# Turning attention probabilities through DRAM instead of on the matrix engine

## The chip, the cores and the metric

One core of a Trainium2 chip runs the kernel. It has a matrix engine (PE, TensorE; its weight loads are listed as PEld), VectorE (DVE), ScalarE (ACT), GpSimd (POOL) and SyncE (SP), each with its own instruction stream, which it works through in order, and 16 DMA engines. The metric is the time of one execution on the device in microseconds (us), the median of several runs.

## The reference

A gated cross-attention followed by a gated mixture of experts, all in float32. x is 8 batches of 256 tokens of width 256, the context 8 batches of 120 rows.

```python
x = x + tanh(g_xattn[0]) * xattn(layernorm(x), ctx_1024, w_q, w_kv, w_out, b_out)
x = x + tanh(g_ffn[0]) * ffn(layernorm(x), W1, W2, Wr)

# xattn: 16 heads of 64
attn = einsum('bnhd,bmhd->bhnm', q, k) * 64 ** -0.5
attn = softmax(attn, axis=-1)
out = einsum('bhnm,bmhd->bnhd', attn, v).reshape(b, n, INNER) @ w_out + b_out

# ffn: 8 experts of width 1024, the 2 best of each token, weighted
h = silu(einsum('btd,efd->btef', x, W1)); y = einsum('btef,edf->bted', h, W2)
out = einsum('bte,bted->btd', gate, y)
```

## The kernel before

There are two phases. **Attention** (up to about 272 us of the span) runs a loop of 32 units, line 1101. Unit s is a batch b (8 of them), a half o of the heads (8 heads) and a half nb of the batch's tokens (128), and k = 2 o + nb is its place in the batch. **Experts** (the rest) first takes one tile of 128 tokens for each expert (the "first" tiles), then full tiles and quarters; the order is the list at line 1061.

A unit's attention goes through these steps. `scores` (line 549) multiplies queries and keys into a PSUM tile psc of two banks, takes the maximum of each of 8 heads on VectorE (line 563), scales it by the negated score factor (line 569), and lets ScalarE write the exponentials into pr, with their sums in sm (line 575). `divide` (line 582) takes the reciprocal of the sums and multiplies pr by it, both on VectorE. `turn_pr` (line 588) turns pr, whose partitions are tokens, into pT, whose partitions are context rows: 8 transposes on PE against an identity matrix into two PSUM tiles tr (line 594), and two copies by ScalarE (line 595). `weigh(b, o)` (line 597) multiplies values by pT for both token halves (tile po), and `wide_out` (line 615) multiplies its result by the output weights (tile pw) for half of the tokens.

The order of the work on PE, VectorE, ScalarE and SP is the order in which the program writes it down (`manual_schedule`, line 417); GpSimd's is not written by hand. In iteration s of the loop, PE gets: the scores of unit s+1; at k=0 `weigh(b-1, 1)`, at k=2 `weigh(b, 0)` and half of the wide_out of the batch before; a part of the projections of queries, keys and values for the next batch (`project_q`, tile pq; `project_k` and `project_kk`, tile pk, copied to kT by VectorE; `project_v`, tile pv); at k=1 the other half of the wide_out and, in every second batch from 3 on, the router's logits (tile plT); at the end the 8 transposes of unit s itself. So the turning of a unit stands right ahead of the scores and the weighing of the next iteration. At k=0 `turn_y` and at k=3 `turn_x` turn normalized rows on PE (tiles lnT), and VectorE copies them; that copy is the last thing VectorE does in iteration k=0, and adding wide_out's result to x (line 626) the last at k=2.

The router's lists lie in DRAM (`routed`, 8 lists of 2048 rows of 265 numbers, one list for an expert). At the start SP fills each of them with empty rows, one transfer for a list of 2.1 MB (line 438). `places` (line 302) computes the rows of tokens and sends them there by indirect DMAs from GpSimd (line 366), two for each step of a generator, from iteration 14 on. Experts' weights are loaded into a buffer w_sb of 8 slabs, one for an expert, each loaded by `load_expert` (line 407) as two DMAs of 1 MB; before they come, the slabs hold attention's weights and intermediate tiles (lines 99 to 105). Expert 0 is loaded at the end of batch 2, 1 of batch 3, 2 of batch 4, and 6, 5, 4, 3 and 7 at the end of attention and in the first iterations of the expert loop. `load` (line 810) brings a first tile by nine DMAs on SP (lines 845 and 852), and the four iterations of the last batch load four of them.

PSUM has 8 banks: two for tr, two for psc (one buffer), four for the projections.

Of the kernel before, what the change touches and what calls it, by code (L numbers as in the profile page):

```python
# [9 lines left out]
F32 = mybir.dt.float32  # L10
I32 = mybir.dt.int32
AF = mybir.ActivationFunctionType
# [37 lines left out]
def tile_gated_xattn_moe(  # L50
# [22 lines left out]
    fp = ctx.enter_context(tc.tile_pool(name="ffn", bufs=2))  # L73
    ps_tr = ctx.enter_context(
        tc.tile_pool(name="ps_tr", bufs=2, space=bass.MemoryType.PSUM)
    )

    attention = ExitStack()
    ap = attention.enter_context(tc.tile_pool(name="attn", bufs=2))
    ps_big = attention.enter_context(  # L80
        tc.tile_pool(name="ps_big", bufs=1, space=bass.MemoryType.PSUM)
    )
# [5 lines left out]

    routed = tc.dram_tile([E * T + P, XW], F32, name="routed")


# [8 lines left out]
    v_sb = [w_sb[:M, 4, ts(i, INNER)] for i in range(2)]  # L100
    pT_sb = part(4, 2 * INNER, 8, N)[:M]
    qT_sb = [part(5, i * IC * N, IC, N) for i in range(2)]
# [39 lines left out]
    for e in range(E):  # L142
        nc.vector.memset(octal[:, e : e + 1], float(E**e))
    empty = w_sb[:, 2, :XW]
    nc.vector.memset(empty, 0.0)
# [156 lines left out]
    def places(g, rows, picked, bank):  # L302
# [56 lines left out]
        for h in range(2):  # L359
            for slot, oh in zip(slots, (oh1, oh2)):  # L360
# [4 lines left out]
                for i in range(2 * h, 2 * h + 2):  # L365
                    send = nc.gpsimd.indirect_dma_start(  # L366
                        out=routed[:, :],
                        out_offset=bass.IndirectOffsetOnAxis(
                            ap=slot[:, i : i + 1], axis=0
                        ),  # L370
                        in_=rows[h][:, i % 2, :],
                        in_offset=None,
                    )


                    for other in sends:
                        tc.declare_no_dep(
                            send.ins, other.ins, reason="each row of a list is sent once"
                        )

                    for first in firsts if g >= EARLY else []:
                        tc.declare_no_dep(
                            send.ins, first.ins, reason="rows behind those of the first tiles"
                        )
                    sends.append(send)
                    if g >= EARLY:
                        behind.append(send)
                yield


    ctxT_sb = ap.tile([P, DC, B * M], F32, name="ctxT_sb", bufs=1)

    x_v = x.rearrange("(n p) d -> p n d", p=P)
# [42 lines left out]
    nc.sync.dma_start(wr_sb[:, :, :E], wrT.rearrange("(c p) e -> p c e", p=P))  # L436
    for e in range(E):
        nc.sync.dma_start(
            routed[ts(e, T), :].rearrange("(n p) w -> p n w", p=P),
            empty.unsqueeze(1).to_broadcast([P, NBLK, XW]),  # L440
        )
    nc.sync.dma_start(routed[ds(NOWHERE, P), :], empty)

# [77 lines left out]
    def project_q(b, xnT, h):  # L521
        pq = ps_mm.tile([P, 2, N], F32, tag="mm", name=f"pq_{b}_{h}")
        for i in range(2):
            for c in range(DC):
# [6 lines left out]
                )  # L531
        nc.scalar.copy(qT_sb[b % 2][:, ts(h, 2), :], pq)

# [15 lines left out]
    def scores(u):  # L549
# [3 lines left out]
        for i in range(4):  # L553
            for j in range(2):
# [6 lines left out]
                )  # L561
        mx = small.tile([P, 8], F32, tag="mx", name=f"mx_{b}_{o}_{nb}")
        nc.vector.tensor_reduce(  # L563
            mx.rearrange("p (j i) -> p j i", i=4),
            psc[:, :, : 4 * M].rearrange("p j (i m) -> p j i m", m=M),
            AX.X,
            ALU.max,
        )
        nc.vector.tensor_scalar(mx, mx, -QK_SCALE, None, ALU.mult)  # L569
        pr = ap.tile([P, 8, M], F32, tag="pr", name=f"pr_{b}_{o}_{nb}", bufs=3)  # L570
        sm = small.tile([P, 8], F32, tag="sm", name=f"sm_{b}_{o}_{nb}")
        for j in range(2):
            for i in range(4):
                h = 4 * j + i
                nc.scalar.activation(  # L575
                    pr[:, h, :], psc[:, j, ts(i, M)], AF.Exp,
                    bias=mx[:, h : h + 1], scale=QK_SCALE,
                    accum_out=sm[:, h : h + 1],
                )
        return pr, sm  # L580

    def divide(pr, sm):
        nc.vector.reciprocal(sm, sm)
        nc.vector.tensor_tensor(  # L584
            pr, pr, sm.unsqueeze(2).to_broadcast([P, 8, M]), ALU.mult
        )

    def turn_pr(u, pr, sm):

        b, o, nb = u  # L590
        for j in range(2):
            tr = ps_tr.tile([P, 4, P], F32, tag="tr", name=f"tr_{b}_{o}_{nb}_{j}")
            for i in range(4):
                nc.tensor.transpose(tr[:M, i, :], pr[:, 4 * j + i, :], ident)  # L594
            nc.scalar.copy(pT_sb[:, ts(j, 4), ts(nb, P)], tr[:M, :, :])  # L595

    def weigh(b, o, ps_mm):

        for h in range(2):
            po = ps_mm.tile([P, 2, N], F32, tag="mm", name=f"po_{b}_{o}_{h}")  # L600
            for k in range(2):
                i = 2 * h + k
                for j in range(2):
                    nc.tensor.matmul(
                        po[ts(j, DH), k, :],
                        lhsT=v_sb[b % 2][:, ts(2 * (4 * o + i) + j, DH)],
                        rhs=pT_sb[:, 4 * j + i, :],
                        start=True,
# [472 lines left out]

    idle = ps_tr.tile([P, 4, P], F32, tag="tr", name="idle")
    for _ in range(10):
# [7 lines left out]
    for h in range(2):  # L1091
        project_q(0, xnTs[0], h)
    prs = {0: scores(units[0])}
    project_k(0, 1)()
    norm_x(1)
    project_q(0, xnTs[0], 2)
    project_v(0, 0)
    divide(*prs[0])
    nc.scalar.activation(tg, tg, AF.Tanh)

    for s, (b, o, nb) in enumerate(units):
        k = 2 * o + nb
        n = b + 1
        g = b // 2 - 1
        routing = b > 1 and b % 2 == 1
        if s + 1 < len(units):
            prs[s + 1] = scores(units[s + 1])

        if s == 0 or k == 2 and b + 2 < B:
            norms_x.finish()  # L1110
        if k == 0 and b > 1:
            norms_y.finish()
        if k == 1 and b + 2 < B:
            if b > 1:
                xs[b + 2] = load_x(b + 2)
            norm_x(b + 2)
        if k > 1 and b > 0:
            norm_y(b - 1, k - 2)


        copies, sums = [], []
        if k == 0 and b > 0:
# [4 lines left out]
        if k == 2:  # L1127
            weigh(b, 0, ps_mm)
            if b > 0:
                sums.append(wide_out(b - 1, 1, ps_mm))  # L1130
        if k == 0:
            project_q(b, xnTs[b], 3)
            if n < B:
                project_v(b, int(b == 0))
        elif n < B:
            project_q(n, xnTs[n], k - 1)
        if k == 1:
            copies += next_k(b, 0)
            if routing and n < B:
# [3 lines left out]
            if routing and n == B:  # L1143
                lg = next(lg)
        if k == 3:
            copies += next_k(b, 1)
            if b > 0:
                project_v(b, 1)
            if n == B - 1:
                project_v(n, 0)  # L1150
        if b == 1 and k % 2 == 0:
            copies.append(project_kk(2, k))
        for copy in copies:
            copy()
        if s + 1 < len(units):
            divide(*prs[s + 1])
        if k == 0 and b > 1:
# [25 lines left out]
        if n == B and k == 3:  # L1183
            open_tile(order[0], xts[0])
            picked[g] = router(g, lg)
        turn_pr((b, o, nb), *prs.pop(s))
        if k == 3 and b + 2 < B:
            turn_x(b + 2)
        if s == 0:
            turn_x(1)  # L1190
        if k == 3 and b in (2, 3, 4):
            load_expert(b - 2)
        if k == 3 and n == B:
            load_expert(6)
# [4 lines left out]


    for name, kw in (
        ("fw", {}),
# [146 lines left out]
```

## Time and profile before

| What | us |
|---|---|
| median of 3 runs (535.99 to 539.37) | 538.03 |
| profiled execution | 538.17 |
| its span | 536.5 |

| Engine | in the attention phase, 150 to 180 us | whole span |
|---|---|---|
| PE | 30.00 of 30 | 520.5 (97%) |
| VectorE | 18.03 | 285.0 (53%) |
| ScalarE | 16.57 | 219.4 (41%) |
| GpSimd | 7.93 | 127.4 (24%) |

The span is the time from the first to the last instruction of the profiled execution. Busy times are sums of an engine's instructions. PE's instructions overlap one another, so that the time that a group of matmuls takes from the rest is better read from the distance between the starts of groups than from their durations. In an answer on the order of time each line has start, duration, engine, line of the program, operation, output and input tiles and count, and in brackets how long the engine had been idle before it and what ended that. In groups by line the numbers behind the count are busy time, mean ns of one, and idle time before them with what ended it.

### The profile page before, as it was taken

The page shows a single profiled execution, that of the slowest core. Times are in us where ns is not written, and L with a number is a line of the kernel's source. Part 1 is how long each engine was busy: PE and PEld are TensorE (multiplying, and loading weights), DVE is VectorE, ACT ScalarE, POOL GpSimd, SP SyncE. Part 2 cuts the span into 40 slices and gives each one's busy share as a digit, 9 for nine tenths or more (in the row PEclk, how much of TensorE's full clock was granted, in tenths as well). Part 3 has the DMA queues.
Part 4 walks back from the last instruction along what each step waited for, and adds up shares of the span by engine and source line. Part 5 has one row for each costly group of instructions (what it writes and reads, how often), then busy time and mean ns, then how long its engine had stood idle before and what let it go on. Part 6 is the DMA issues. An engine that isn't in the chain of part 4 may idle for free. (4 is left out here: it accounts for less than half of the span.)

```text
span 536.5 us, 10501 instructions
## 1 busy us (share of the span) xinstructions
PE 520.5 (97%) x3636; PEld 439.3 (82%) x3636; DVE 285.0 (53%) x683; ACT 219.4 (41%) x700; POOL 127.4 (24%) x135
## 2 busy tenths in 40 slices
PE   8999999999999999999999999899999999999992
PEld 7788887878878788787889998799997787889991
DVE  3675656567765577644673446344544454443530
ACT  1666546464654655557530302011144555601110
POOL 2011100000332003310013446122331224333332
PEclk9999999999999999999999999899999999999998
DMA  8999990140521501012059784333332221332321
GB/s 295 336 305 306 309 254 21 49 148 2 169 88 35 184 1 40 32 47 35 2 179 375 224 244 74 42 42 44 48 44 32 31 33 16 49 36 26 43 28 20
DMA packets 82157, 57.58 MB, mean 107 GB/s; under 512 B 42864, under 2 KB 77168, under 8 KB 82096
## 3 DMA queue, kind: packets, MB, share of 16 engines
q1 hardware_dynamic: 75200, 47.36, 32.0%
q0 software_dynamic: 6480, 8.81, 9.1%
q10 hardware_dynamic: 416, 0.66, 0.4%
q8 instruction: 30, 0.49, 0.4%
q14 instruction: 31, 0.25, 0.2%
HBM read 28.67 MB, written 28.27 MB: 106 GB/s over the span
## 5 line engine op out<-in xcount | busy, mean ns | idle before, releaser
L575 ACT ACTIVATE pr<-psc,mx 128x120 f32<-128x120 f32 x256 | 88.2, 370 | 65.4 <-DVE mx L569 63.3
L897 PEld LDWEIGHTS ph_full<-xT_full,w 128*128 128x128 f32 x736 | 86.6, 195 | 8.7 <-issue 7.4
L897 PE MATMUL ph_full<-xT_full,w 128*128 128x128 f32 x736 | 88.5, 279 | 2.3 <-DVE xT_full L884 2.0
L913 PE MATMUL py_full<-w,hT_full 128*128 128x256 f32 x368 | 83.1, 379 | 0.0
L913 PEld LDWEIGHTS py_full<-w,hT_full 128*128 128x128 f32 x368 | 68.2, 190 | 8.4
L905 ACT ACTIVATE hT_full<-ph_full 128x1024 f32<-128x1024 f32 x23 | 23.5, 1022 | 98.0 <-PE ph_full L897 92.0
L525 PE MATMUL pq<-xnT,w_sb 128*128 128x256 f32 x256 | 62.7, 388 | 0.4 <-DVE xnT L208 0.4
L938 POOL DMA_INDIRECT out_dram<-y_full,xt_full x23 | 39.2, 1705 | 100.1 <-DVE y_full L921 69.9
L619 PE MATMUL pw<-w_sb 128*128 128x256 f32 x256 | 58.5, 382 | 0.0
L575 ACT ACTIVATION_READ_ACCUMULATOR pr<-psc,mx 128x1 f32 x256 | 55.5, 217 | 0.0
L525 PEld LDWEIGHTS pq<-xnT,w_sb 128*128 128x128 f32 x256 | 46.6, 190 | 10.8 <-issue 3.1
L619 PEld LDWEIGHTS pw<-w_sb 128*128 128x128 f32 x256 | 47.7, 190 | 9.0 <-issue 2.5
L563 DVE TENSOR_REDUCE mx<-psc 128x8 f32<-128x960 f32 x32 | 37.0, 1156 | 31.4 <-PE psc L555 31.4
L366 POOL DMA_INDIRECT routed<-rows,slot x32 | 31.9, 995 | 55.6 <-DVE slot L362 48.9
L921 DVE TENSOR_SCALAR y_full<-py_full,gate 128x256 f32<-128x256 f32 x23 | 11.1, 484 | 60.3 <-PE py_full L913 54.9
L595 ACT COPY w_sb<-tr 120x512 f32<-120x512 f32 x64 | 34.6, 596 | 20.0 <-PE tr L594 20.0
L584 DVE TENSOR_TENSOR pr<-pr,sm 128x960 f32<-128x960 f32 x32 | 37.1, 1158 | 1.1
L555 PE MATMUL psc<-kT,w_sb 64*128 64x120 f32 x512 | 37.2, 284 | 0.0
L985 ACT COPY part<-w_sb 128x1024 f32 x32 | 31.0, 1043 | 13.5 <-PE py_q L1024 13.0
L555 PEld LDWEIGHTS psc<-kT,w_sb 64*128 64x128 f32 x512 | 31.1, 187 | 6.4 <-issue 3.6
L864 DVE COPY w<-w_sb 128x2048 f32 x23 | 29.0, 1259 | 12.0 <-issue 4.9
L594 PEld LDWEIGHTS tr<-ident,pr 128*120 128x120 f32 x256 | 29.5, 138 | 5.7 <-issue 3.1
(173 smaller groups left out, 648.8 us busy)
## 6 DMA issues: line engine op xcount, KB each, us to landing
routed<-w_sb SPq DMA_DIRECT2D x8, 2120.0 KB
w_sb<-in_w1T_dram SPq DMA_DIRECT2D x8, 1024.0 KB
w_sb<-in_w2T_dram SPq DMA_DIRECT2D x8, 1024.0 KB
xt_full<-routed SPq DMA_DIRECT2D x184, 16.0 KB
out_dram<-x SPq DMA_DIRECT2D x8, 256.0 KB
x<-in_x_dram SPq DMA_DIRECT2D x7, 256.0 KB
w_sb<-in_w_kv_dram SPq DMA_DIRECT2D x3, 512.0 KB
w_sb<-in_w_q_dram SPq DMA_DIRECT2D x2, 512.0 KB
```

Of the source, the lines that this page charges most:

```text
L366: send = nc.gpsimd.indirect_dma_start(out=routed[:, :], out_offset=bass.IndirectOffsetOnAxis(ap=slot[:, i : i + 1], axis=0), in_=rows[h][: ...
L525: nc.tensor.matmul(pq[:, i, :], lhsT=wq_sb[:, c, ts(2 * h + i, P)], rhs=xnT[:, c, :], start=(c == 0), stop=(c == DC - 1),)
L555: nc.tensor.matmul(psc[:, j, ts(i, M)], lhsT=qT[ts(j, DH), 4 * o + i, ts(nb, P)], rhs=kT[ts(j, DH), 4 * o + i, :], start=True, stop=True,)
L563: nc.vector.tensor_reduce(mx.rearrange("p (j i) -> p j i", i=4), psc[:, :, : 4 * M].rearrange("p j (i m) -> p j i m", m=M), AX.X, ALU.max,)
L575: nc.scalar.activation(pr[:, h, :], psc[:, j, ts(i, M)], AF.Exp, bias=mx[:, h : h + 1], scale=QK_SCALE, accum_out=sm[:, h : h + 1],)
L584: nc.vector.tensor_tensor(pr, pr, sm.unsqueeze(2).to_broadcast([P, 8, M]), ALU.mult)
L595: nc.scalar.copy(pT_sb[:, ts(j, 4), ts(nb, P)], tr[:M, :, :])
L619: nc.tensor.matmul(pw[:, :D], lhsT=oT_sb[b % 2][:, ci, ts(k, P)], rhs=wo_sb[:, ci, :], start=(ci == 0), stop=(ci == IC - 1),)
L897: nc.tensor.matmul(ph[:, f, :], lhsT=w1[:, c, ts(f, P)], rhs=xT[:, c, :], start=(c == 0), stop=(c == DC - 1),)
L913: nc.tensor.matmul(py[:, :D], lhsT=hT[:, f, :], rhs=w2[:, f, :], start=(f == 0), stop=(f == FC - 1),)
L938: add = nc.gpsimd.indirect_dma_start(out=out[:, :], out_offset=bass.IndirectOffsetOnAxis(ap=slots[:, k : k + 1], axis=0), in_=y[own, :], i ...
L985: nc.scalar.copy(w[:, q, :].rearrange("p (a b) -> p a b", b=D if down else DFF // 2), slab[:, ts(h, FC // 2), :] if down else slab[:, :, t ...
```

## The change

Probabilities are no longer turned on PE. Each pr is now a tile of its own for a token half, padded with zeros from 120 to 128 columns. `divide` keeps the reciprocal on VectorE and gives the multiplication to GpSimd. `turn_pr` turns pr in blocks of 32 x 32 on VectorE into a tile `blocks`, and SP sends it with four DMAs of 128 KB to a DRAM tile, where the blocks are put in their places. A new step `fetch_pr` at the end of the same iteration brings the turned 512 KB back into pT with one DMA on SP. pT now has two buffers, one for each half of the heads, in the slabs of experts 2 and 4.

The scores are computed two units ahead instead of one, in two buffers of psc (the banks that tr had). The queries are scaled and negated as they are copied, so that a minimum takes the place of the maximum and no scaling follows it. `scores` has become a generator: the exponentials of one bank of psc are issued in one iteration, those of the other at the start of the next.

In an iteration the projections and the copies of keys now come first, then the block transpose with its DMAs, then the scores of unit s+2, and then weigh and wide_out. The lists are filled by 32 DMAs of 0.54 MB, one in each iteration, each of 64 rows of all 8 lists. Expert 2 is loaded in the last iteration of attention. At the end of an iteration SP's order is: first tile of the last batch if any, fill, expert if any, fetch.

```diff
-    for e in range(E):
-        nc.sync.dma_start(
-            routed[ts(e, T), :].rearrange("(n p) w -> p n w", p=P),
-            empty.unsqueeze(1).to_broadcast([P, NBLK, XW]),
-        )
+    def fill_lists():
+        n = T // B // 4
+        j = len(fills)
+        fill = nc.sync.dma_start(
+            routed[: E * T, :].rearrange("(e n r) w -> n r e w", e=E, r=n)[j],
+            empty[:n].unsqueeze(1).to_broadcast([n, E, XW]),
+        )
...
-        nc.scalar.copy(qT_sb[b % 2][:, ts(h, 2), :], pq)
+        nc.scalar.mul(qT_sb[b % 2][:, ts(h, 2), :], pq, -QK_SCALE)
...
     def divide(pr, sm):
         nc.vector.reciprocal(sm, sm)
-        nc.vector.tensor_tensor(
-            pr, pr, sm.unsqueeze(2).to_broadcast([P, 8, M]), ALU.mult
-        )
+        nc.gpsimd.tensor_tensor(
+            pr[:, :, :M], pr[:, :, :M], sm.unsqueeze(2).to_broadcast([P, 8, M]), ALU.mult
+        )
...
-    def turn_pr(u, pr, sm):
+    def turn_pr(u, pr):
         b, o, nb = u
-        for j in range(2):
-            tr = ps_tr.tile([P, 4, P], F32, tag="tr", name=f"tr_{b}_{o}_{nb}_{j}")
-            for i in range(4):
-                nc.tensor.transpose(tr[:M, i, :], pr[:, 4 * j + i, :], ident)
-            nc.scalar.copy(pT_sb[:, ts(j, 4), ts(nb, P)], tr[:M, :, :])
+        nc.vector.transpose(
+            blocks.rearrange("p k h s -> p h k s"),
+            pr.rearrange("p h (k s) -> p h k s", s=BLK),
+        )
+        for q in range(P // BLK):
+            nc.sync.dma_start(
+                turned_pr[nb][:, ts(q, 8 * BLK)].rearrange("(k r) w -> r k w", r=BLK),
+                blocks[ts(q, BLK)].rearrange("r k h s -> r k (h s)"),
+            )
+
+    def fetch_pr(u):
+        b, o, nb = u
+        nc.sync.dma_start(
+            pT_sb[o][:, nb].rearrange("p q h s -> p (q h s)"), turned_pr[nb]
+        )
...
-                        rhs=pT_sb[:, 4 * j + i, :],
+                        rhs=pT_sb[o][:M, :, :, 4 * j + i, :].rearrange(
+                            "p n q s -> p (n q) s"
+                        ),
...
+        pr, sm = probs
+        divide(pr, sm)
         if s + 1 < len(units):
-            prs[s + 1] = scores(units[s + 1])
+            probs = next(exps[s + 1])
...
+        for copy in copies:
+            copy()
...
+        if s + 2 < len(units):
+            exps[s + 2] = scores(units[s + 2])
+        turn_pr((b, o, nb), pr)
+        if s + 2 < len(units):
+            next(exps[s + 2])
...
-        turn_pr((b, o, nb), *prs.pop(s))
...
-        if k == 3 and b in (2, 3, 4):
+        if len(fills) < T // 64:
+            fill_lists()
+        if k == 3 and b in (2, 3):
             load_expert(b - 2)
+        if k == 3 and n == B:
+            load_expert(2)
+        fetch_pr((b, o, nb))
         if k == 3 and n == B:
             load_expert(6)
```

## The prediction

> **What bounds the kernel now.** I read the page's busy times first, then the groups by line, then the order of time on the matrix engine, and last the two queues of the new path.
>
> ```profile
> PE 520.5 (97%) x3636; PEld 439.3 (82%) x3636; DVE 285.0 (53%) x683; ACT 219.4 (41%) x700; POOL 127.4 (24%) x135
> PE   8999999999999999999999999899999999999992
> ```
>
> PE is busy in every slice: only work that leaves PE, or a wait that PE gets, moves the end. The groups that the change touches:
>
> ```profile
> L584 DVE TENSOR_TENSOR pr<-pr,sm 128x960 f32<-128x960 f32 x32 | 37.1, 1158 | 1.1
> L594 PE MATMUL tr<-ident,pr 128*120 128x128 f32 x256 | 33.2, 273 | 0.0
> L459 POOL TENSOR_TENSOR x<-x,bias_sb 128x512 f32<-128x512 f32 x8 | 10.1, 1266 | 43.0 <-DVE xn L197 34.5 <-DVE bias_sb L1176 8.5
> L884 DVE STREAM_TRANSPOSE xT_full<-xt_full 128x256 f32<-128x256 f32 x23 | 10.0, 436 | 1.5 <-DMA xt_full<-routed 0.8 <-issue 0.3 <-DVE gate L869 0.3
> ```
>
> Durations overlap on PE, so its prices are differences of starts (batch 5, order of time, PE):
>
> ```profile
> 185.16 1.99 PE L525 MATMUL pq<-xnT,w_sb 128*128 128x256 f32 x8
> 186.99 1.88 PE L537 MATMUL pv<-w_sb,ctxT_sb 128*120 128x512 f32 x4
> 188.70 0.60 PE L207 MATMUL lnT_f<-ident,rows 128*128 128x128 f32 x4
> ...
> 191.76 1.99 PE L525 MATMUL pq<-xnT,w_sb 128*128 128x256 f32 x8
> 193.60 1.78 PE L499 MATMUL pk<-ctxT_sb,w_sb 128*128 128x240 f32 x8
> 195.22 0.27 PE L231 MATMUL pl<-ident,lgT 128*128 128x128 f32 x1
> 195.32 3.62 PE L619 MATMUL pw<-w_sb 128*128 128x256 f32 x16
> 198.78 1.04 PE L594 MATMUL tr<-ident,pr 128*120 128x128 f32 x8
> 199.75 1.16 PE L555 MATMUL psc<-kT,w_sb 64*128 64x120 f32 x16
> 200.83 1.95 PE L604 MATMUL po<-w_sb 120*64 120x256 f32 x16
> 202.71 3.72 PE L619 MATMUL pw<-w_sb 128*128 128x256 f32 x16
> ```
>
> So pq 1.83, pv 1.71, pk 1.62, pw 3.46, tr 0.97, psc 1.08, po 1.88 us; lnT 0.5 and the router's plT 0.57 come from the same view, elsewhere. Nothing separates them: no gap is there to be closed. On the sync queue and at a small load's landing:
>
> ```profile
> 275.30 0.41 SPq L411 DMA_DIRECT2D w_sb<-in_w2T_dram  x1
> ...
> 284.02 12.03 SPq L845 DMA_DIRECT2D xt_first<-routed  x8
> ...
> 336.94 0.35 SPq L852 DMA_DIRECT2D xt_full<-routed  x1
> ...
> 338.65 0.15 DVE L869 COPY gate<-xt_full 128x1 f32 x1 [4.76 <-DMA xt_full<-routed]
> ```
>
> Eight block loads that take 3.9 us to issue elsewhere took 12.03 behind expert loads: what is behind bulk on this queue waits for it. A small load lands 1.33 us after its issue ends (337.29 to 338.62).
>
> **What leaves PE.** 32 units x 0.97 = 31.0 us. Also gone: 34.6 us of L595 copies on ACT (41% busy: worth nothing) and on DVE the division (37.1) and the scaling of the maximum (5.7), which the new block transposes replace: 436 ns is 256 elements plus some 0.17, so 1024 take 1.24; 32 x 1.24 = 39.7. DVE stays even. The fills leave the start of SP's queue, where they issue from 15.8 to 72.6 us; nobody on PE waits there, so 0. The padded rows, the second score buffer and the late opening of the transpose pool cost 0, hidden by PE work before their first use (if that cover fails, about one psc, 1.1 us). Weighing reads runs of 32; no row shows such a read: 0 taken, 0 to 3 us (a tenth of the 31.3 us po group).
>
> **What comes on the path.** Before, a unit's turning was PE's own work just ahead of the weighing that reads it. Now unit s goes reciprocal, POOL, DVE, four writes to DRAM, one fetch, inside one iteration, and the weighing stands in the next one. PE issues in order: what is queued behind that weighing (its own second half, wide_out, the next projections) waits too. Two such laps per batch count: k=1 (read at k=2) and k=3 (read at k=0).
>
> T, from PE's start of the iteration to the end of the block transpose: the reciprocal stands on DVE behind the last copy of the iteration before, which waits for PE's last matmul there (lnT_f or pw), so it ends at about 1.05 to 1.35. POOL: 1266 ns for 512 elements, so 2.37 for 960; done at 3.5 to 3.85. But kT's copy stands ahead of the transpose: pq 1.83 + pk 1.62 + 0.2, copy 0.66, so 4.35; transpose 1.25: **T = 5.6** (4.8 to 5.15 where no kT is left, in batches 6 and 7; 7.55 for the two pq of unit 1). Where the router's sends are queued on POOL ahead of the division (two at 0.96 plus 0.3 each, after their slots), T grows by 2.8 at k=3 of batches 3 and 5 and by 2.0 at k=1 of 4 and 6; 0 to these values.
>
> R, from there to the landing: four issues at 0.43 with gaps 1.85; the write's landing 1.33 (the load above) to 2.65 (an indirect add to DRAM to the wait behind it, 379.43 to 382.09): 1.7, nearer to the plain load; fetch issue 0.4; landing 1.33 plus 512 KB at 375 GB/s, 1.4; half a microsecond for waits and the fill or x ahead of it: **R = 7.0**. From below: issues at 0.38, landing 1.33, half of the data hidden, 5.6; from above 2.65 and all of the 0.54 MB fill and 0.26 MB of x ahead, 8.4.
>
> The Trainium skill (DMA: Bandwidth & Descriptors, Anatomy of one DMA) puts 2.0 us fixed plus bytes by 436 GB/s on a DMA, and most of it on the receipt from DRAM; as an estimate the lap is 1.3 + 2.3 + 3.2 = 6.8 and the sum 3 us less; no row shows such a write.
>
> PE's cover, from the iteration's start to the weighing: k=1: pq+pk+psc+pw = 8.0, then pq+psc 2.9: 10.9 (11.6 with the router, batches 3 and 5). k=3: pq+pk+pv+psc+lnT 6.74, then pq+pv+psc 4.62: 11.4. Stall = T + R - cover:
> - batch 0: 14.55-9.4 = 5.1 (no pw yet) and 1.3; batch 1: 0.1 and 1.2
> - batches 2 to 5, k=1: 1.7, 1.0, 3.7, 1.0; k=3: 1.2 each, with the sends 2.8 in 3 and 5, and 6.5 in 2 and 3, where load_expert (2.1 MB at 300 to 375 GB/s: 5.6 to 7.0) is issued ahead of the fetch: 7.7, 10.5, 1.2, 4.0
> - batch 6, with no kT and little behind it: 14.65-9.3 = 5.4, and 11.8-7.4 = 4.4
> - batch 7: nine first loads (4.2 us of issue) stand between write and fetch, R = 9.7: 5.15+9.7-5.3 = 9.5. At the end expert 2, moved from batch 4 to here, stands there too, R = 16: 4.8+16-5.4 (pv, the first up) = 15.4
>
> Beside the path: the exponentials of unit s+2 write the pr that the transpose of s reads, so ACT waits for T; the scores they read have a second buffer and are used two iterations later, so 0 (else half a unit's exponentials, 1.35). SP now waits for each transpose and each write: out stores and x loads behind it come up to one lap later, and are needed a batch later, 0. Expert 2 adds 2.1 MB to the 10.5 of the five loads behind the attention, 5.6 to 7.0 us; PE itself comes 15 to 25 us later there, so 0.
>
> Sum 6.4+1.3+9.4+11.5+4.9+5.0+9.8+24.9 = 73.2, less 31.0: **+42**. The profiled execution took 538.2 (span 536.5), the median is 538.0: 580.
>
> **Clock.** The warm-up matmuls at the start took 421 ns in the median, the last 275: PE is slower after idleness. Nothing is put into the sum for it. The Trainium skill (TensorE: Matmul & The Clock Gate, Why this matters for your kernels) warns of gaps over some 3 us; by its window of 3.4 us at half rate the nine stalls above that would cost up to 9 x 1.7 = 15 us more, an estimate that makes 595; no gap in this trace tests it.
>
> **Rivals.**
> *Short lap* (faster). The queue lets the fetch pass the bulk (no 6.5, three times) and the lap is 4.2 (issues 1.5, 1.33, 0.4, 1.0 left of the load). Stalls: batch 0 2.3, 3 1.2, 4 0.9, 5 1.2, 6 4.2, 7 13.3: 23, so -8: 530; with no stall at all it would be 507. It decides below a lap of about 5.2. For it: 406 GB/s at most at the start, plain loads that land in 1.33. Against: the 12.03 us above, and that two landings and five issues follow one another.
> *Passing queue, medium lap* (no change): R = 5.6 and no waiting behind bulk: stalls 34, +3: 541.
> *Long lap* (slower still): R = 8.4, 16 x 1.4 = 22 more, 602; or POOL's division slower than its row, at 2.37 more each about 35: 615.
> That the transposes stay on PE can't be: the diff leaves none.
>
> **How the numbers follow.** Forecast (R 5.6 to 8.4 with the queue holding: 560 to 602; without half of the sends 5 less) 0.62; long lap over 604: 0.09; no change within 1% (what a measurement can tell apart), 0.12; short lap 0.17, wider than its one number since three prices of the lap (division, write, fetch) have no row of their own. Faster 0.17, same 0.12, slower 0.71. The time is the forecast's, 580. The range takes in no change and most of the short lap, 524 to 606: about 0.1 is left out below and 0.08 above. The forecast's own range is 555 to 604.
>
> **What would show it.** PE busy falls to 84 to 88% of a longer span; L594 is gone. PE's waits are at po, named as pT's fetch, 16 of them, longest in batches 2, 3, 6, 7 and at the first tile. POOL's division takes 2.4 us, the transpose 1.2. From the transpose's end to po some 7 us. It is wrong if po doesn't wait (then T isn't tied to PE's last matmul), or if waits at batches 2 and 3 are like those of 1 and 4 (the queue doesn't hold).

## The result and the profile after

| | median, us | runs | ratio to before |
|---|---|---|---|
| before | 537.22 | 4 (535.99 to 539.37) | |
| after | 653.43 | 4 (652.29 to 658.91) | 1.2178 (95% interval 1.2098 to 1.2259) |

The change makes the kernel 22% slower: +116 us where +42 was forecast. The profiled execution of the changed kernel has a span of 651.4 us against 536.5. Its page, busy times and slices (PEclk is the granted clock of PE in tenths), then the costly groups:

```profile
span 651.4 us, 10190 instructions
...
PE 524.4 (81%) x3380; PEld 427.1 (66%) x3380; DVE 295.9 (45%) x651; ACT 187.8 (29%) x636; POOL 187.1 (29%) x169
...
PE   8968987945947775966862629998999999999993
...
PEclk9979999878988787999866958999999999999998
...
L643 PE MATMUL po<-w_sb 120*64 120x256 f32 x256 | 49.6, 554 | 90.2 <-DMA w_sb<-turned 43.5
...
L612 POOL TENSOR_TENSOR pr<-pr,sm 128x960 f32<-128x960 f32 x32 | 57.4, 1794 | 121.3 <-DVE sm L611 121.0
...
L620 DVE STREAM_TRANSPOSE blocks<-pr 128x1024 f32<-128x1024 f32 x32 | 39.6, 1237 | 28.5 <-POOL pr L612 25.6
```

Three things stand in these lines. The deep holes in PE's row are all in the first 24 slices, the attention, and the weighing (po) has 90.2 us of idle time ahead of it. PE's busy time has not fallen: 520.5 before, 524.4 now, although 31 us of transposes are gone, so what stayed got slower by 34.9 us; po went from 31.3 us to 49.6, pw from 58.5 to 65.2. And the clock row dips to 5 and 6 where the deepest holes are. Windows of 1 us say how much of the 34.9 is the clock: busy time times what the granted clock lacks of 1 adds up to 31.9 us, against 1.7 before. The difference of the spans splits up: -31.0 for the transposes, +111.0 idle time of PE (127.0 instead of 16.0), +34.9 busy time: 114.9.

The waits of PE, by what ended them (total, number, longest):

```profile
PE po L643 <- DMA w_sb<-turned: 43.5, 5, 15.5
PE po L643 <- issue: 23.5, 6, 7.5
PE po L643 <- DMA turned<-blocks: 16.7, 2, 12.2
PE pl L237 <- DVE lgT L234: 13.3, 3, 6.6
PE po L643 <- DVE mn L592: 6.5, 1, 6.5
```

The po lines are one wait under several names: the weighing waits for the fetch (w_sb<-turned); where another event came last by the record, that one is named. They add up to the 90.2. By place, against the forecast:

| batch | wait of `weigh(b, 0)` at k=2, forecast / measured | wait of `weigh(b, 1)` at the next k=0 |
|---|---|---|
| 0 | 5.1 / 6.2 | 1.3 / 1.8 |
| 1 | 0.1 / 1.0 | 1.2 / 2.5 |
| 2 | 1.7 / 3.8 | 7.7 / 9.4 |
| 3 | 1.0 / 0, behind 6.6 at pl | 10.5 / 11.4 |
| 4 | 3.7 / 4.5 | 1.2 / 3.4 |
| 5 | 1.0 / 0, behind 6.6 at pl | 4.0 / 4.6 |
| 6 | 5.4 / 7.5 | 4.4 / 6.5 |
| 7 | 9.5 / 12.2 | 15.4 / 15.5 |
| sum | | 73.2 / 90.2 |

One lap, that of batch 3's last unit, on the sync queue (order of time: start, duration):

```profile
181.99 1.76 SPq L625 DMA_DIRECT2D turned<-blocks  x4
...
184.93 0.66 SPq L424 DMA_DIRECT2D w_sb<-in_w1T_dram  x1
...
187.97 3.02 SPq L632 DMA_DIRECT2D w_sb<-turned  x1
```

The writes are issued at 181.99. Between them and the fetch stand, in the lines left out too, a store, a fill and both halves of expert 1, and the fetch's own issue takes 3.02 us there (0.34 in batch 1). PE gets its data at 198.74, 16.75 us after the first write. What a weighing then looks like (order of time, PE; in brackets the idle time before it):

```profile
97.24 1.95 PE L643 MATMUL po<-w_sb 120*64 120x256 f32 x16 [2.54 <-issue]
...
143.68 3.68 PE L643 MATMUL po<-w_sb 120*64 120x256 f32 x16 [9.35 <-DMA w_sb<-turned]
...
159.54 0.48 PE L237 MATMUL pl<-ident,lgT 128*128 128x128 f32 x1 [6.59 <-DVE lgT L234]
159.81 5.88 PE L660 MATMUL pw<-w_sb 128*128 128x256 f32 x16
```

Behind a wait of 2.5 us the same 16 matmuls take 1.95 us, behind 9.35 us 3.68, and a pw behind 6.59 takes 5.88 instead of 3.72. The wait at pl is a new one, not at po. VectorE around it:

```profile
158.14 0.43 DVE L191 BATCH_NORM_STATS2 st_x<-x 128x6 f32<-128x256 f32 x1 [3.95 <-DMA x<-in_x_dram]
...
159.23 0.26 DVE L234 COPY lgT<-plT 128x128 f32<-128x128 f32 x1
```

The copy that PE waits for stands in VectorE's queue behind statistics of an x tile. That tile's load is issued at 154.98, right behind the four writes at 153.17, which wait for the block transpose.

### The profile page after: what moved, and what is told of

It is laid out like the page before. It is cut to its first block, busy times and chain, and to the rows that moved or that the text cites. A ratio compares the mean times of both kernels' runs of the same rounds, so it can differ in the third digit from the quotient of the medians.

```text
span 651.4 us, 10190 instructions
## 1 busy us (share of the span) xinstructions
PE 524.4 (81%) x3380; PEld 427.1 (66%) x3380; DVE 295.9 (45%) x651; ACT 187.8 (29%) x636; POOL 187.1 (29%) x169
## 5 line engine op out<-in xcount | busy, mean ns | idle before, releaser
L643 PE MATMUL po<-w_sb 120*64 120x256 f32 x256 | 49.6, 554 | 90.2 <-DMA w_sb<-turned 43.5
L603 ACT ACTIVATE pr<-psc,mn 128x120 f32<-128x120 f32 x256 | 88.2, 370 | 114.5 <-DVE mn L592 114.5
L643 PEld LDWEIGHTS po<-w_sb 120*64 120x64 f32 x256 | 26.9, 196 | 105.1 <-issue 102.1
L612 POOL TENSOR_TENSOR pr<-pr,sm 128x960 f32<-128x960 f32 x32 | 57.4, 1794 | 121.3 <-DVE sm L611 121.0
L660 PE MATMUL pw<-w_sb 128*128 128x256 f32 x256 | 65.2, 413 | 0.0
L603 ACT ACTIVATION_READ_ACCUMULATOR pr<-psc,mn 128x1 f32 x256 | 55.5, 217 | 0.0
L652 DVE COPY w_sb<-po 128x512 f32<-128x512 f32 x32 | 21.6, 685 | 71.1 <-PE po L643 71.0
L620 DVE STREAM_TRANSPOSE blocks<-pr 128x1024 f32<-128x1024 f32 x32 | 39.6, 1237 | 28.5 <-POOL pr L612 25.6
L561 ACT ACTIVATE w_sb<-pq 128x512 f32<-128x512 f32 x32 | 19.6, 612 | 83.1 <-PE pq L553 83.1
L592 DVE TENSOR_REDUCE mn<-psc 128x8 f32<-128x960 f32 x32 | 35.9, 1125 | 11.4 <-PE psc L584 11.4
L584 PEld LDWEIGHTS psc<-kT,w_sb 64*128 64x128 f32 x512 | 31.7, 191 | 12.6 <-issue 11.4
```

The costliest lines, as they stand in the source:

```text
L584: nc.tensor.matmul(psc[:, j, ts(i, M)], lhsT=qT[ts(j, DH), 4 * o + i, ts(nb, P)], rhs=kT[ts(j, DH), 4 * o + i, :], start=True, stop=True,)
L592: nc.vector.tensor_reduce(mn.rearrange("p (j i) -> p j i", i=4), psc[:, :, : 4 * M].rearrange("p j (i m) -> p j i m", m=M), AX.X, ALU.min,)
L603: nc.scalar.activation(pr[:, h, :M], psc[:, j, ts(i, M)], AF.Exp, bias=mn[:, h : h + 1], scale=-1.0, accum_out=sm[:, h : h + 1],)
L612: nc.gpsimd.tensor_tensor(pr[:, :, :M], pr[:, :, :M], sm.unsqueeze(2).to_broadcast([P, 8, M]), ALU.mult)
L620: nc.vector.transpose(blocks.rearrange("p k h s -> p h k s"), pr.rearrange("p h (k s) -> p h k s", s=BLK),)
L643: nc.tensor.matmul(po[ts(j, DH), k, :].rearrange("p (q s) -> p q s", s=BLK), lhsT=v_sb[b % 2][:, ts(2 * (4 * o + i) + j, DH)], rhs=pT_sb[o ...
```

## The experiments

My theory after the result: the lap through DRAM is the loss, as waits, and as a slow PE after each wait. Rivals: the strided reads make the weighings slow; single positions in queues (x, the fetch) make most of the waits; bandwidth, not order; or parts of the change beside the route.

**Is PE slow because it had stood idle?** Matmuls without use are put ahead of each weighing and of pl, so many that they last about as long as the wait there.

```diff
             po = ps_mm.tile([P, 2, N], F32, tag="mm", name=f"po_{b}_{o}_{h}")
+            if h == 0:
+                keep_warm(po[:, 0, :P], WARM.get(4 * b + 2 + 2 * o, 0))
```

> The changed kernel with idle work for PE where it waits: before each weighing that waited, as many 128-column matmuls as fill the measured wait less half a microsecond (4 to 131 of them, into the weighing's own PSUM tile, which the weighing overwrites), and 53 before each of the two late router transposes. Nothing else changes. Theory (idleness makes PE slow afterwards): the waits for the fetch stay, but the weighings after them run at 1.9 us instead of 3.6, the wide_out after the router at 3.5 instead of 5.8; the weighings' busy time falls from 49.6 to 31 to 34 us and the time from 653 to 615 to 628. Rival (PE is slow in the weighing because it reads pT in runs of 32 numbers, or because the DMA traffic holds its reads): the weighings stay at 3.6 us and the time at 648 to 656.

703.7 us, ratio 1.3089 (1.3051 to 1.3127): far above both. Each such matmul is two instructions on PE (154 for a count of 77, 17.46 us), so a matmul took 0.23 us and not the 0.11 that I had reckoned with; the work was twice the wait and delayed what it should only have covered. It still shows one thing: every weighing behind it takes 1.95 us and the mean clock is 0.993 (0.904 without). With half the counts:

> The run with idle work for PE again, with half as many matmuls at each place, since each float32 matmul took 0.23 us there and not 0.11, so that the idle work was twice the waits. Theory (idleness makes PE slow): weighings at 1.9 us, no or short waits left before them, PE's busy time without the idle work about 490 us instead of 524; 653 less 30 to 35 plus up to 10 for idle work that is too long: 618 to 632. Rival (the layout that is read, or the traffic, makes the weighing slow): weighings at 3 to 3.7 us again, 650 to 660.

638.1 us, ratio 1.1817 (1.1685 to 1.195), clock 0.984. In its order of time on PE (the first line is the work without use):

```profile
131.04 8.75 PE L643 MATMUL po<-before,ones 128*128 128x128 f32 x76
141.27 1.95 PE L654 MATMUL po<-w_sb 120*64 120x256 f32 x16 [1.48 <-DMA w_sb<-turned]
...
343.12 3.36 PE L654 MATMUL po<-w_sb 120*64 120x256 f32 x16 [5.60 <-DMA w_sb<-turned]
```

The weighing that waited 9.35 us and took 3.68 takes 1.95 when PE has been kept at work, and the one that still waits 5.60 takes 3.36. So idleness is the cause of the slow matmuls. Keeping PE at useless work makes the kernel 15 us faster, less than the 21 to 35 that I expected. In the profiled executions PE's busy time without the useless work falls from 524.4 to 499.2 us, but what is idle or useless grows from 127.0 to 139.9: of the 25 us won, 13 go into longer waits, since a PE that is done sooner waits longer for the same lap.

**The waits at po taken away altogether.** All weighings but the last read a constant tile.

```diff
-                        rhs=pT_sb[o][:M, :, :, 4 * j + i, :].rearrange(
+                        rhs=(pT_sb[o] if b == B - 1 and o else still)[
+                            :M, :, :, 4 * j + i, :
+                        ].rearrange(
```

> The changed kernel, but all weighings except the last one read a tile of zeros of pT's shape and layout in the free half of slab 2, instead of pT; the block transposes, the writes and the fetches all run. So attention adds only its bias, except in the last batch's second half. Theory (the laps' waits, and the slowness behind them, are the loss): no wait before the weighings of the loop, about 15 us at the first tile, some 15 to 21 us for the late x loads stay; 537 less 31 plus 30 to 40: 536 to 555. Rival (91 MB of DMA, the block transposes and GpSimd's division slow the other engines): 575 or more, with waits at other places in place of those. Rival (reads in runs of 32 are slow): weighings stay near 554 ns a matmul though nothing waits.

603.7 us, ratio 1.123 (1.1188 to 1.1272): 50 us less, not 100, as the rival said. PE's waits:

```profile
PE pl L241 <- DVE lgT L238: 18.9, 2, 11.3
PE po L647 <- DMA w_sb<-turned: 18.5, 1, 18.5
```

and VectorE's in the same run:

```profile
DVE blocks L624 <- DMA turned<-blocks: 23.6, 5, 7.0
DVE blocks L624 <- POOL pr L616: 23.0, 8, 4.3
...
DVE st_x L195 <- DMA x<-in_x_dram: 20.9, 4, 6.4
```

Nobody on PE reads the turned probabilities any more, and PE still waits: the block transpose sits in VectorE's queue, waits there for GpSimd's division and for the writes of the unit before to leave the one blocks tile, and the copies that PE needs (lgT, xnT, po's) stand behind it. The strided read itself costs nothing: a weighing takes 1.95 us with runs of 32 as with whole rows before the change.

**x loaded one iteration earlier, and the fetch ahead of the bulk.** Two runs, each with one position on SP's queue changed.

```diff
-            if b > 1:
-                xs[b + 2] = load_x(b + 2)
             norm_x(b + 2)
...
         fetch_pr((b, o, nb))
+        if k == 0 and 1 < b < B - 2:
+            xs[b + 2] = load_x(b + 2)
```

> The changed kernel with the load of x for batch b+2 issued one iteration earlier, behind the fetch of k=0, instead of at k=1 just ahead of the statistics that read it. Theory: VectorE's waits for x (18.5 us) and PE's two waits of 6.6 us for the router's logits go to under 1 us, and the slow wide_out behind them (5.8 us) with them; but the weighings at k=2 of batches 3 and 5, which waited for nothing because PE was already late, get waits of 2 to 5 us: 653 less 10 to 16, 637 to 643. Rival (what PE gains there it loses wholly at the next weighing): 650 to 655.

642.9 us, ratio 1.1959 (1.1915 to 1.2003); the waits at pl go from 6.6 to 2.5 each. The time is inside the range, and the x load is the cause of the larger part of these waits, but they were to go under 1: 2.5 us have another cause (see the last 19 us below). The waits of 2 to 5 us that I expected at k=2 of batches 3 and 5 didn't come.

```diff
+        fetch_pr((b, o, nb))
         if n == B:
             xts[k] = load(order[k])
...
-        fetch_pr((b, o, nb))
```

> The changed kernel with the fetch issued ahead of the first tiles' loads, the fill and the experts of its iteration instead of behind them. Theory (the queue holds the fetch behind bulk): from the fetch's issue to the weighing 3 us instead of 4.2; the waits at batches 2 and 3 of k=0 fall from 9.4 and 11.4 to 3 to 5, that at k=2 of batch 7 from 12.2 to 7 to 9, at the first tile from 15.5 to 7 to 10, and each of the others by about 1: 35 to 45 us of waits, and 8 to 15 less of slow matmuls behind them: 595 to 612. Rival (transfers of one queue don't hold one another, the lap is all latency): the waits at batches 2 and 3 stay, 640 to 653.

627.7 us, ratio 1.1676 (1.1642 to 1.171): in the right direction, but 16 us short of the range.

```profile
130.68 1.95 PE L643 MATMUL po<-w_sb 120*64 120x256 f32 x16 [1.39 <-issue]
...
151.37 0.48 PE L237 MATMUL pl<-ident,lgT 128*128 128x128 f32 x1 [13.14 <-DVE lgT L234]
```

The waits of batches 2 and 3 fall from 9.35 to 1.39 and from 11.40 to 2.90: being issued behind the bulk was their cause. But the expert that now comes behind the fetch holds up the next unit's writes and the x load, and pl waits 13.14 instead of 6.59. A first tile now waits 10.1 us for an expert's w1T as well.

**A whole iteration more for the lap.** Division, block transpose and fetch of unit s+1 move into iteration s.

```diff
-        turn_pr((b, o, nb), pr)
+        if s + 1 < len(units):
+            turn_pr(units[s + 1], probs[0])
...
-        fetch_pr((b, o, nb))
+        if s + 1 < len(units):
+            fetch_pr(units[s + 1])
```

> The changed kernel with each unit divided, turned, written and fetched one iteration earlier, unit s+1 in iteration s, with the same instructions. The lap then has some 7 more us of PE's work before its weighing. Theory (the lap's waits and the cold PE behind them are the main loss, the rest are VectorE's waits for x and for the block tile on the one queue): the waits before the weighings fall from 90 us to 5 to 20, what is left at batches 2, 3 and 7; the waits for x stay or grow (15 to 30 us): 575 to 600, a little under the kernel whose weighings read constants (604). Rival (the path from the scores to the fetch has no slack at all, so that an earlier turning only moves the wait to the reciprocal, which now stands right behind the exponentials): 630 to 655.

609.9 us, ratio 1.1294 (1.1226 to 1.1363), above the range. The waits at po fall from 90.2 to 19.6, and others come: 20.0 at pl, 14.4 for xnT, 11.4 for w1T, 9.1 for copies that free a PSUM tile. VectorE in that run:

```profile
DVE blocks L620 <- POOL pr L612: 50.7, 23, 3.7
...
DVE blocks L620 <- DMA turned<-blocks: 17.3, 4, 6.9
```

**Fills and experts on ScalarE's DMA queue.**

```diff
-        fill = nc.sync.dma_start(
+        fill = nc.scalar.dma_start(
...
-            load_expert(b - 2)
+            load_expert(b - 2, nc.scalar)
```

> The changed kernel with the 32 fills and the experts 0, 1 and 2 issued from ScalarE's queue instead of SP's, at the same places of the program. Theory (order within one queue holds the fetch; two queues share the engines): the waits at batches 2 and 3 of k=0 fall from 9.4 and 11.4 to 4 to 6, at the first tile by 4 to 6, the others by 1 each: 653 less 25 to 40: 613 to 630. Rival (bandwidth holds it, not order): 640 to 653.

653.8 us, ratio 1.2108 (1.205 to 1.2165): nothing gained, close to the rival's 640 to 653. The waits of batches 2 and 3 are 7.13 and 9.49 (9.35 and 11.40 on one queue), and SP now waits 64.5 us for the landing of the writes, against 43.4. In batch 2 the second half of the expert is issued beside the fetch here (132.84 to 134.85, the fetch at 132.99) and not ahead of it, and still the data are there only 9.2 us after the fetch's issue, as on one queue (9.1). That fits transfers that share the 16 DMA engines whatever their queue; no run separates it further. It helps to issue the fetch first (the run above), not to issue the bulk elsewhere.

**All of it together:** turning ahead, bulk on ScalarE's queue, x early, two blocks tiles, the fetch ahead of the first loads.

> Four edits together: turning one unit ahead, fills and experts 0 to 2 on ScalarE's queue, x loaded one iteration earlier, two block tiles, and the fetch ahead of the first tiles' loads. Theory: no wait before a weighing over 2 us, none for x, PE not slow; 537 less 31 plus 5 to 25 for what stays in the last batch and of contention: 511 to 535, faster than the kernel before. Rival (the traffic of 91 MB and GpSimd beside VectorE set a bound of their own): over 560.

603.1 us, ratio 1.1169 (1.1037 to 1.13): the best with the route, but 64 us over the kernel before and far above the range, as the rival had it. Left are 15.9 at pl, 14.2 at the first tile's po, 13.6 for xnT; the block transposes wait 58.3 us for GpSimd's division (32.6 and 25.7 in the two tiles). But for the first tile and one wait of 3.9 us the lap is out of PE's way by then, and VectorE's queue has taken its place.

**The route alone undone.** PE transposes into the same pT, everything else of the change kept.

```diff
-        turn_pr((b, o, nb), pr)
...
-        fetch_pr((b, o, nb))
+        turn_pr((b, o, nb), pr)
...
+                nc.tensor.transpose(tr[:M, i, :], pr[:, 4 * j + i, :M], ident)
```

> Only the route is undone: unit s is turned by 8 PE transposes at the end of its iteration, ScalarE copies them into the same pT, and there are no block transposes, no writes and no fetch (a third pr buffer keeps the exponentials of s+2 away from the transposes). GpSimd's division, scores two ahead, the new order, the fills in 32 pieces and the late expert 2 stay. If the lap through DRAM, with what it puts on VectorE's and SP's queues, is the whole loss: 532 to 545 us, PE busy 518 to 524 at a clock over 0.98, idle under 25, waits at po under 3 in all. Rival, that the late expert 2, the fills in pieces or GpSimd's division cost of their own: 555 to 640, with waits at ph_first for w1T, at xnT, or at tr for GpSimd.

556.6 us, ratio 1.0343 (1.0313 to 1.0374). Replacing the route saves 97 of the 116 us. The other 19 are the rival's; in the changed kernel itself the first of the two waits below isn't seen, since PE comes too late there to wait for that expert. PE's waits:

```profile
PE ph_first L930 <- DMA w_sb<-in_w1T_dram: 10.5, 1, 10.5
PE pl L237 <- DVE lgT L234: 4.1, 2, 2.0
```

**GpSimd's division** was tried on both sides, with VectorE's old one put back into the last run and into the changed kernel.

```diff
-        nc.gpsimd.tensor_tensor(
+        nc.vector.tensor_tensor(
```

> As the run with PE transposes, with the division on VectorE as before. If GpSimd's division costs PE nothing there: within 3 us of that run (530 to 545), L203 back at about 410 ns from 860 to 1090. Rival, that VectorE beside GpSimd is slow enough to hold PE: over 5 us less.

556.1 us, ratio 1.0339 (1.0306 to 1.0372): the same as with GpSimd.

> The changed kernel with the division alone back on VectorE (the route through DRAM stays). T at k=1 is set by the copy of kT, so nothing there; behind the router's sends (k=3 of batches 3 and 5) T falls from 7.8 to 5.5, in batches 6 and 7 by 0.5: 640 to 650 us, waits at po 80 to 87, L203 at about 410 ns. Rival, that GpSimd's division holds the lap or VectorE everywhere: under 630.

649.1 us in its one run, waits at po 83.6: inside the range. By this one run the division's engine is worth some 4 us of the 116.

**The last 19 us.** Expert 2 back at batch 4, with one pT tile for both halves, and x loaded at k=0.

```diff
-        for e, off in ((2, 0), (4, 2 * INNER))
+        for e, off in ((4, 2 * INNER),) * 2
...
-        if k == 3 and b in (2, 3):
+        if k == 3 and b in (2, 3, 4):
```

> As the run with PE transposes, with expert 2 loaded at the end of batch 4 again (both halves of pT use the one tile in slab 4, as before the change) and x of two batches on loaded at k=0 instead of k=1. That run was 18.7 us above the kernel before; its waits were 10.5 for w1T at a first tile and 4.1 at pl, and the clock was 0.81 from 300 to 330 us. If the move of expert 2 is what remains: the 10.5 and the slow clock go, 536 to 543 us, idle 15 to 19. Rival, that the fills in pieces, which now share the DMA engines with the experts' loads, or GpSimd's division hold something too: 545 to 556, with the wait at ph_first still there.

553.2 us, ratio 1.0277 (1.0238 to 1.0316), as the rival had it: the wait for w1T is halved and not gone, and pl still waits 2.0 twice, so x isn't what it waits for here. Then, with the fills at the start of the queue as well:

```diff
         fills.append(fill)
+    for _ in range(T // 64):
+        fill_lists()
```

> As the last run (PE transposes, expert 2 and x in their places), with all 32 pieces of the lists' fill issued at the start of SP's queue, where the fills stood before the change. Left there: 15.7 us over the kernel before, 5.0 of it a wait for w1T at a first tile. If the fills in pieces hold the experts' loads: the wait at w1T under 1, 540 to 548. Rival, that they only moved bytes and the rest is the new order of the iteration: 551 to 556, the wait still there.

559.7 us, ratio 1.0419 (1.0385 to 1.0452): neither. The wait for w1T is gone, as it should be if the fills in pieces had held the experts' loads, but another has come. PE and SP in order of time:

```profile
116.79 1.11 PE L625 MATMUL tr<-ident,pr 128*120 128x128 f32 x4 [8.09 <-POOL pr L614]
```

```profile
16.29 79.79 SPq L460 DMA_DIRECT2D routed<-empty  x32
...
109.89 0.39 SPq L419 DMA_DIRECT2D x<-in_x_dram  x1
```

The 32 fills hold SP until 96 us; an x load is issued at 109.89, VectorE waits 15.66 us for it, and the reciprocal for GpSimd's division stands behind that. The x load itself stands behind a store that is issued only at 96.19.

What the 19 us consist of is shown in part. Up to 10.5 are the expert that comes late: 5.5 of them went with its move back, the other 5.0 with the fills. The rest is that PE comes later to the first expert tile, at 281.6 us in the run with expert 2 in its place against 271.8 before the change. Of these 9.7 us, 6.3 are more idle time of PE, 4.1 of it the two waits at pl, and 3.4 are more busy time. The first of these waits, in that run:

```profile
129.41 0.64 PE L226 MATMUL plT<-xn2T,wr_sb 128*32 128x128 f32 x16
132.08 0.30 PE L237 MATMUL pl<-ident,lgT 128*128 128x128 f32 x1 [2.03 <-DVE lgT L234]
132.22 5.31 PE L652 MATMUL pw<-w_sb 128*128 128x256 f32 x16
```

Before the change two projections stood between plT and pl (191.19 and 195.22 us), in the new order of the iteration nothing does, so PE waits while VectorE makes lgT; the pw behind it takes 5.31 us instead of 3.62. That the order is the cause is read from the trace and not tested by a run. No version made here beats the kernel before.

## Why the prediction was wrong

**What held.** The kernel got slower through the mechanism forecast: the weighing waits for its own unit's fetch, at fourteen of the sixteen places (at the other two PE had already waited at pl), and the order of the waits by batch is as worked out, with the longest in batches 2, 3, 7 and at the first tile. T was right: 5.4 to 5.5 us in batches 1 and 2 against 5.6, 7.8 behind the router's sends against 8.4. Bulk issued ahead of the fetch does hold it (1.39 and 2.90 us with the fetch first), and not only on the one queue: with the bulk on ScalarE's the waits stay at 7.13 and 9.49. PE's share fell to 81%, a little below the 84 to 88 named. The block transpose took 1.24 us as priced. The division took 1.79 and not 2.37, which changed little, because the copy of kT stands ahead of the transpose (the run with VectorE's division on the route took 649.1).

**Three steps failed.**

*"Clock. ... Nothing is put into the sum for it."* This is the largest error. A term that I had worked out was put at nothing. I named it, worked out 15 us by the rule of the Trainium skill (TensorE: Matmul & The Clock Gate, Why this matters for your kernels: no gaps over some 3 us) and left it out because no gap in the trace before tested it. Here eleven weighings behind waits of 3.4 us or more take 3.35 to 3.68 us instead of 1.95, and PE's remaining work grew by 34.9 us in all, 25.0 of it in the groups po and pw, and 30 of it by the granted clock. The page's window of 3.4 us at half rate agrees with these rows; my estimate by it was less than half of the growth. It counted nine gaps, and there are eleven of this kind and two more at pl, each with a slow pw behind it; and it charged 1.7 us for a gap, while the clock often stays at half for longer than the weighing (behind 3.76 us of waiting the next pw, too, takes 4.67 us instead of 3.72). As a limit the 3 us don't hold: in the run with x early a wait of 1.95 us is followed by a weighing of 3.45.

*R = 7.0.* The term was mis-sized. Batch 1, with only a fill beside the lap, on SP and then on PE:

```profile
68.55 1.76 SPq L625 DMA_DIRECT2D turned<-blocks  x4
...
72.34 0.34 SPq L632 DMA_DIRECT2D w_sb<-turned  x1
```

```profile
76.86 1.95 PE L643 MATMUL po<-w_sb 120*64 120x256 f32 x16 [1.02 <-DMA w_sb<-turned]
```

From the first write's issue to po it was 8.3 us here, 8.2 to 10.3 in the ten plain laps, and 16.75 behind an expert (13.5 by the forecast's sum). The write's landing was priced at 1.7 and took about 2.0. The larger part is the fetch: from its issue's end at 72.68 to po 4.2 us, where I had put 2.7. Over the fourteen laps that PE waited for, R came out some 37 us longer than priced. That the sum of the waits is only 17 us too low (73.2 and 90.2) is partly luck: T was shorter than priced in the last batches (4.0 instead of 4.8), and PE's cover longer, most at the first tile (8.9 instead of 5.4, with another wait in it). The sum for R was also added up wrongly: its terms give 7.2, and those of its upper bound 9.8 with the fetch's own 1.4 in it, not 8.4; 9.8 would have covered most plain laps. The landing of 1.33 is 1.36 by the row shown (338.65), and batch 6 at k=1 comes to 14.15 by the T given there, not 14.65. An estimate of the lap by the Trainium skill (DMA: Bandwidth & Descriptors, Anatomy of one DMA) had been lower still, 6.8; the page's fit is for transfers that GpSimd issues, and these are SP's.

*"out stores and x loads behind it come up to one lap later, and are needed a batch later, 0."* The wait was put at nothing. The loads are used in the same iteration: `norm_x` puts their statistics into VectorE's queue ahead of the copy of the router's logits. PE waits 6.6 us twice at pl, which the run with x early takes down to 2.5; what is left fits the new order, where pl follows plT at once. I looked for who reads x on PE, a batch later, and not for what is queued behind its first reader.

The forecast is 73 us short of the difference of the spans. The three make up 65 of them: 34.9 for the slow PE, 17.0 for the waits at po, 13.3 at pl.

**What the sum couldn't have shown in one pass.** Even with all waits at po gone but the last the kernel takes 604 us, and with a whole iteration more for the lap 610. The prediction looked at one path, PE's weighing. VectorE's in-order queue is a second one: with a reciprocal in it that waits for ScalarE and a transpose that waits for GpSimd and for DMAs, all copies for PE behind them wait too. So of the rivals, the one on the slower side (*long lap*, 602 to 615) came nearest, and too low as well; *short lap* and *passing queue* fell, since the bulk does hold the fetch and the lap is longer than 7 us.

## What to carry to other kernels

Before moving work from a saturated in-order engine onto a chain of others, write down for each engine of the chain what is queued behind its waiting instruction and who reads that: here the waits came back on VectorE's copies as soon as they left the weighing. A wait on PE of some 2 to 3 us or more can cost twice, once as a gap and once as matmuls at half speed behind it (1.95 us of waiting did in one run); a cheap engine-local transpose of 1 us per unit was worth keeping. When a transfer has to be early, issue it ahead of the bulk; a second queue for the bulk didn't do it.

## What the runs showed of the hardware

- Idleness costs PE half its speed: a weighing behind a long wait takes 3.68 us instead of 1.95, at a granted clock of 0.50. It can outlast the weighing: the clock is 0.50 from 114.5 to 120 us and from 387 to 396, and 1.00 from 120 to 122. By windows of 1 us there are thirteen such stretches up to 420 us, idle time included, of 3.4 to 20.5 us, each near a multiple of 3.4. The length of wait that brings it on isn't sharp. In the changed kernel weighings behind waits up to 2.54 us take 1.95 us, behind 3.40 us and more 3.35 to 3.68; but in the run with x early one behind 1.95 us is slow, and in the run with the fetch ahead one behind 2.93 us isn't:

```profile
60.55 3.45 PE L643 MATMUL po<-w_sb 120*64 120x256 f32 x16 [1.95 <-issue]
```

```profile
272.60 1.95 PE L643 MATMUL po<-w_sb 120*64 120x256 f32 x16 [2.93 <-issue]
```

- Useless work ahead of the wait keeps the granted clock at 0.984 instead of 0.904 and the kernel at 638.1 instead of 653.4 us.
- VectorE is slowed by GpSimd's division. Its normalization of 128x256 takes 407 ns in the mean with the division on VectorE, and beside GpSimd's 858 for xn and 1093 for rows. VectorE and GpSimd of the changed kernel, in order of time:

```profile
71.96 2.16 DVE L203 TENSOR_SCALAR xn<-x,mv_x,rstd_x 128x256 f32<-128x256 f32 x2
```

```profile
72.12 1.85 POOL L612 TENSOR_TENSOR pr<-pr,sm 128x960 f32<-128x960 f32 x1 [0.39 <-DVE sm L611]
```

The pair, which takes 0.73 us in the run with PE transposes and VectorE's division, takes 2.16 here and ends 0.15 us after the division does. The Trainium skill (SBUF — State Buffer, SBUF: two separate sides) says that the two engines share a port pair, which VectorE uses only for some of its instructions and which one of them holds for a whole instruction, and the rows agree. It cost little here: 556.6 and 556.1 us with either engine where PE transposes, 653.4 and 649.1 with the route.
- Bulk moved to a second DMA queue of the core still delayed the fetch: 9.35 and 11.40 us of wait became 7.13 and 9.49, where issuing the fetch ahead of it on the one queue gave 1.39 and 2.90.
